# Projections kept in DRAM: pieces of 256 tokens split into pieces of 128, and the slot stores issued from ScalarE

## The chip, the cores and the metric

One core of one Trainium2 chip runs the kernel. The metric is the device time of a run in microseconds (us). A time named "median" is that of repeated runs; the profile is of one further execution, recorded by the hardware profiler. The engines are TensorE (PE; its weight loads are PEld), VectorE (DVE), ScalarE (ACT), GpSimd (POOL) and SyncE (SP). SyncE here only issues DMAs; ScalarE and GpSimd can issue DMAs too. Each engine carries out its own instructions in the order of the program.

## The reference, cut to what matters

Four sequences ("elements", b = 0 to 3) of 1024 tokens with 256 features pass through two layers, each an attention and a feed-forward part, with a normalisation after each. The change touches the first attention only:

```
x = _layernorm(x + _L0_attn_ref(x, ...))          # 16 heads of 16 features
    qkv = einsum('bsc,oc->bso', x, w_qkv)         # the projections
    q = layer_norm(q); k = layer_norm(k)          # per head, then rotary positions
    out = softmax(q k^T / 4) v, then w_proj
x = _layernorm(x + _L0_ffn_ref(x, ...))
x = _layernorm(x + _L1_attn_ref(x, ...))          # causal, 8 heads
x = _layernorm(x + _L1_ffn_ref(x, ...))           # 16 experts, 2 per token, 512 slots each
```

The last part scatters token rows into expert slots; slots that no token fills must hold an empty row.

## The kernel before, in words

All data is float32. The first attention of an element is written as 64 *units* (`first_units`): four groups of four heads, 16 steps each. A step i computes scores of the current group (`Attend.head`, L459) and, side by side, scores of the next group for its row maxima only (`Maxima.head`, L435). Four heads of 16 features (padded to 32) share the array at a time. A unit has two sets of four such products; between them come the value products of the step before (L477), and at some steps four transposes (L426, L492). Each score tile takes one of six PSUM banks (pool `ps_s`). ScalarE frees a score bank by the exponential (L468), VectorE frees a maxima bank by a reduction (L438). A seventh bank (`ps_m`, one buffer) serves transposes and all other products of this stage.

The order of the work is written by hand. `weave(units, n, pieces, big, mid, at, side, ...)` runs through the units, and behind each unit it does, in this order: `tick()`, which runs steps that were put off by `later(n, fn)` for n ticks; one step of `side`; then as many of `pieces` as bring `done` up to `total * (u + 1) // n`. From unit `at` on an entry of `mid` takes the place of the pieces once. For the first element (b = 0) this call has

- as units the 64 of `first_units(0)`;
- as pieces two empty ones and then the *stash*: the projections of elements 1, 2 and 3, which are made here and kept in DRAM until their turn. `stash_qk(b, pr)` makes queries and keys of half the heads (pr 0 and 1), `stash_v(b)` the values of b = 2 and 3. Order: qk(1,0), qk(1,1), v(2), qk(2,0), qk(2,1), v(3), qk(3,0), qk(3,1), four pieces of 256 tokens each, 32 in all;
- as mid `load_heads(1, 0)` at unit 30, which loads kept projections back;
- as side `prep`, one step per unit: loads of x (units 0 to 7), small weight steps on VectorE (`geometric`, units 8 and 9), the empty rows (made at unit 11, stored to the slots of expert e at unit 15 + e by `empty_slots`, L1210; a further store to `acc_d` at unit 27, L1213), and three integer weights: load of wg at unit 28, GpSimd's conversions (L1155) at 30 to 33, wu at 34 and 36 to 39, wd at 40 and 42 to 45. The empty rows and all three integer weights share one buffer ("hT").

A stash piece loads its input (`load_xin`, L140, tile "xin" with two buffers) on SyncE's queue, makes eight product instructions of 128x256 (four matmuls; L299 for qk, L331 for v) in the bank of `ps_m`, and ScalarE copies the bank out (L307, L339). For qk, one tick later GpSimd squares the copy (L311), two ticks later VectorE sums it (L313), and three ticks after the fourth piece SyncE stores 1 MB of projections (L316) and 64 KB of sums (L317). The 1 MB tile "va1" has one buffer, the sums' tile has two. For v, one tick after each piece SyncE stores its 256 KB (L340); that tile has two buffers. SyncE's queue thus holds, in program order, input loads, stores that wait for ScalarE or VectorE, slot stores, and weight loads that wait for GpSimd. `load_heads` also puts eight steps of about 2.9 us (L357) on GpSimd, one per tick.

Of the kernel before, what the change touches and what calls it, by code (L numbers as in the profile page):

```python
# [10 lines left out]
F32 = mybir.dt.float32  # L11
# [8 lines left out]
P = 128  # L20
# [15 lines left out]
def postln_layers_kernel(ctx: ExitStack, tc: tile.TileContext, a: dict, out: bass.AP):  # L36
    nc = tc.nc
# [65 lines left out]
    with ExitStack() as main:  # L103
# [4 lines left out]
        act = main.enter_context(tc.tile_pool(name="act", bufs=1))  # L108
# [8 lines left out]
        def later(n, fn):  # L117
            due.append((now_at[0] + n, fn))
# [12 lines left out]
        def bank(name, big):  # L131

            if big:
                return ps_s.tile([P, 512], F32, tag="s", name=name)
            return ps_m.tile([P, 512], F32, tag="m", name=name)

        def load_xin(b, j, name):
            t = fa.tile([P, 2, 256], F32, tag="xin", bufs=2, name=f"xin{name}_{b}_{j}")
            lo = b * S + j * 256
            nc.sync.dma_start(t, a["xT"][:, lo : lo + 256].rearrange("(c p) n -> p c n", p=P))  # L140
            return t
# [140 lines left out]
        for b in range(1, B):  # L282
            v_d[b] = dram.tile([P, TB * C], F32, name=f"v_d{b}")
            for pr in range(2):
                qk_d[b, pr] = dram.tile([P, TB * 256], F32, name=f"qk_d{b}{pr}")
                ss_d[b, pr] = dram.tile([P, TB * 16], F32, name=f"ss_d{b}{pr}")

        def stash_qk(b, pr):
            kept = {}

            def piece(j, big):
                if j == 0:
                    kept["x"] = act.tile([P, TB * 256], F32, tag="va1", bufs=1, name=f"xs_{b}_{pr}")
                    kept["ss"] = act.tile([P, TB * 16], F32, tag="k1", bufs=G1, name=f"sss_{b}_{pr}")
                xin = load_xin(b, j, f"k{pr}")
                ps = bank(f"qk0_{b}_{pr}_{j}", big)
                for i in range(2):
                    for c in range(2):
                        nc.tensor.matmul(  # L299
                            ps[:, i * 256 : (i + 1) * 256],  # L300
                            xin[:, c, i * P : (i + 1) * P],
                            w0[:, c, pr * 256 : (pr + 1) * 256],
                            start=c == 0,
                            stop=c == 1,
                        )
                x = kept["x"][:, j * 512 : (j + 1) * 512]
                nc.scalar.copy(x, ps)  # L307

                def squares():
                    sq = act.tile([P, 512], F32, tag="q1", bufs=G1, name=f"sqs_{b}_{pr}_{j}")  # L310
                    nc.gpsimd.tensor_tensor(sq, x, x, ALU.mult)  # L311
                    ss = kept["ss"][:, j * 32 : (j + 1) * 32]
                    later(1, lambda: nc.vector.tensor_reduce(ss, sq.rearrange("p (h d) -> p h d", d=D0), AX.X, ALU.add))  # L313

                def store():
                    nc.sync.dma_start(qk_d[b, pr], kept["x"])  # L316
                    nc.sync.dma_start(ss_d[b, pr], kept["ss"])  # L317

                later(1, squares)
                if j == 3:  # L320
                    later(3, store)

            return [lambda big, j=j: piece(j, big) for j in range(4)]

        def stash_v(b):
            def piece(j, big):
                xin = load_xin(b, j, "v")
                ps = bank(f"v0_{b}_{j}", big)
                for i in range(2):
                    for c in range(2):  # L330
                        nc.tensor.matmul(  # L331
                            ps[:, i * 256 : (i + 1) * 256],
                            xin[:, c, i * P : (i + 1) * P],
                            w0[:, c, 512:768],
                            start=c == 0,
                            stop=c == 1,
                        )
                x = act.tile([P, 512], F32, tag="nmT", bufs=2, name=f"vs_{b}_{j}")
                nc.scalar.copy(x, ps)  # L339
                later(1, lambda: nc.sync.dma_start(v_d[b][:, j * 512 : (j + 1) * 512], x))  # L340

            return [lambda big, j=j: piece(j, big) for j in range(4)]

        def load_heads(b, pr):

            xr = fa.tile([P, TB, 2, 8, D0], F32, tag="xr", bufs=1, name=f"xr_{b}_{pr}")
            ss = fa.tile([P, TB, 2, 8], F32, tag="ss", bufs=1, name=f"ss_{b}_{pr}")
            heads[b, pr] = (xr, ss)
            flat = ss.rearrange("p t s h -> p (t s h)")
            nc.sync.dma_start(flat, ss_d[b, pr])  # L350
            nc.sync.dma_start(xr.rearrange("p t s h d -> p (t s h d)"), qk_d[b, pr])

            def roots(k):
                if k == 0:
                    nc.gpsimd.tensor_scalar(flat, flat, D0 * 1e-6, None, ALU.add)
                p = flat[:, 16 * k : 16 * k + 16]
                nc.gpsimd.tensor_tensor(p, p, neg_half.to_broadcast([P, 16]), ALU.pow)  # L357

            for k in range(8):
                later(1 + k, lambda k=k: roots(k))  # L360
# [644 lines left out]
        def first_units(b):  # L1005

            oq0[b] = act.tile([P, TB, C], F32, tag="oq", bufs=2, name=f"oq0_{b}")
            last = None
            for g in range(G0):
                n = 4 * b + g  # L1010
                at = Attend(groups[n], oq0[b])
                mx = groups.get(n + 1)
                for i in range(16):
                    for hp in range(2):

                        then = []
                        for j in range(2):
                            if mx is not None:
                                then += [at.head(i, 2 * hp + j), mx.head(i, 2 * (1 - hp) + j)]
                            elif hp == 0:  # L1020
                                then += [at.head(i, 2 * j), at.head(i, 2 * j + 1)]
                        for fn in then:
                            fn()
                        if hp == 0:
                            if i > 0:
                                at.values(i - 1)
                            elif last is not None:
                                last.values(15)
                            if i == 3:
                                groups[n].turn(0, 1, name="a")  # L1030
                            if i == 5 and last is not None:
                                last.unload(1)
                            if i == 10 and mx is not None:
                                mx.turn(0, 0, name="a")
                            if i == 11:
                                at.unload(0)
                            if i >= 12 and n + 2 in groups:
                                groups[n + 2].turn((i - 12) // 2, i % 2)
                    if i == 0:
                        groups[n].close(1)  # L1040
                    if i == 3 and n + 2 < G0 * B:
                        nb, ng = divmod(n + 2, G0)
                        groups[n + 2] = Maxima(nb, ng, both_pool)
                    if i >= 4 and n + 2 in groups:
                        groups[n + 2].rotate(4)
                    if i == 8 and mx is not None:
                        mx.close(0)
                    yield
                last = at
            last.values(15)  # L1050

            def end(big):
                last.unload(1, big)

            ends[b] = end
# [145 lines left out]
        def empty_slots(e):  # L1201
            if e < 0:
                empty["z"] = z = act.tile([P, ECH, ROW], F32, tag="hT", bufs=1, name="empty")
                nc.gpsimd.memset(z, 0.0)
                none = act.tile([P, ECH], I32, tag="v_none", bufs=1, name="none")
                nc.gpsimd.iota(none, pattern=[[P, ECH]], base=N, channel_multiplier=1)
                nc.gpsimd.tensor_copy(z[:, :, ROW - 1].bitcast(I32), none)
            elif e < EM:
                to = disp_d[e * CAP : (e + 1) * CAP, :].rearrange("(c p) d -> p c d", p=P)
                nc.sync.dma_start(to, empty["z"])  # L1210
            else:
                rest = acc_d[N : N + CAP, :].rearrange("(c p) d -> p c d", p=P)
                based.append(nc.sync.dma_start(rest, empty["z"][:, :, 0:C]).ins)  # L1213
# [36 lines left out]
        for b in range(1, B):  # L1250
            stash += (stash_v(b) if b > 1 else []) + stash_qk(b, 0) + stash_qk(b, 1)
        weave(
            first_units(0), 64, [wait, wait] + stash, False, [lambda big: load_heads(1, 0)], 30, [f for f in prep if f], 0
        )
        flush()
        straight(project_v(1))
# [261 lines left out]
```

## Time and profile before

| | us |
|---|---|
| median of 3 runs | 2520.82 (2514.46 to 2523.96) |
| the profiled execution | 2506.56 |
| its span, first to last instruction | 2504.9 |
| TensorE busy in it | 2362.7 (94%) |
| VectorE, ScalarE, GpSimd busy | 1327.1, 1022.9, 740.7 |
| units of the first element, second value products to last | 95.95 to 410.68 |

In a timeline a line holds the start, the time until the end of the last instruction merged into it, the engine (SPq is SyncE's queue), the source line, the operation, the tile written and the tiles read, the shape, how many instructions were merged (x8), and in brackets the idle time before it with what ended it. Products overlap, since four of the small ones share the array, so their starts say more than their lengths.

In the stretch from 95 to 412 us the costliest groups of instructions are the maxima and score products (L435, L459), 503 records each; VectorE is busy 59% of the time from 95.95 to 410.68 and ScalarE 55% (186.82 and 172.40 of 314.73).

### The profile page before, as it was taken

Reading aid. Unit: us, or ns where it says so; the run is one execution under the profiler, and the core shown is the slowest. Engines: PE = TensorE matmul, PEld = TensorE weight load, DVE = VectorE, ACT = ScalarE, POOL = GpSimd, SP = SyncE. Lnnn points to the kernel's source line nnn. Section 1 sums busy time; section 2 is a strip of 40 time slices with the busy share of each in tenths; the row PEclk is TensorE's granted clock in tenths of the full one; section 3 lists DMA queues with packets and bytes.
Section 4 is the critical chain, followed back from the end, with each engine's and each line's share of the span. In section 5 each row is a group of like instructions: output and inputs, shape, how many; then the busy total and the mean of one; then the engine's idle time right before and its main releaser. Section 6 shows DMA issues by size and latency. Waiting matters only on the chain.

```text
span 2504.9 us, 36507 instructions
## 1 busy us (share of the span) xinstructions
PE 2362.7 (94%) x14452; PEld 1193.4 (48%) x14452; DVE 1327.1 (53%) x2945; ACT 1022.9 (41%) x2011; POOL 740.7 (30%) x1047
## 2 busy tenths in 40 slices
PE   6999999999999999999999999999999994999994
PEld 3333344444445544444455444445556443666662
DVE  6765554766656537687564566816534555111113
ACT  1355454555452345545524555462342340111112
POOL 5623622525124113454041320210111053112223
PEclk8999999999998999999989999999999895999997
DMA  3134223000000000001000000102000012444434
GB/s 88 34 112 134 70 68 100 1 27 1 1 1 27 2 1 1 23 30 48 31 1 1 1 1 1 52 18 98 1 1 1 1 52 68 101 101 118 103 89 145
DMA packets 79771, 109.89 MB, mean 44 GB/s; under 512 B 8944, under 2 KB 68592, under 8 KB 77936
## 3 DMA queue, kind: packets, MB, share of 16 engines
q1 hardware_dynamic: 54080, 80.21, 9.7%
q0 software_dynamic: 9984, 14.82, 3.1%
q10 hardware_dynamic: 15536, 12.53, 1.7%
q8 instruction: 113, 1.85, 0.3%
q14 instruction: 58, 0.48, 0.1%
HBM read 68.64 MB, written 38.90 MB: 43 GB/s over the span
## 4 chain that ended last, share of the span: by engine, by line
PE 85%; DVE 6%; POOL 4%; DMA 2%; issue 1%; ACT 1%; ACTq 0%; SPq 0%; POOLq 0%; DVEq 0%
PE sc L459 19%; PE av L477 9%; PE ph L1379 7%; PE py L1395 7%; PE gu L604 7%; PE sc L932 4%; PE mx L435 4%; PE mx L885 4%; PE p L852 4%; PE dn L620 3%; PE av L969 3%; PE dn L969 2%; PE ppa L568 2%; DVE part L896 2%; PE qk L299 2%; PE pt L426 1%
## 5 line engine op out<-in xcount | busy, mean ns | idle before, releaser
L438 DVE TENSOR_REDUCE part<-mx 128x1 f32<-128x512 f32 x1024 | 657.0, 685 | 355.0 <-PE mx L435 349.4
L468 ACT ACTIVATE pe<-sc 128x512 f32<-128x512 f32 x1024 | 554.0, 596 | 391.1 <-PE mx L435 333.3
L435 PE MATMUL mx<-kT,qT 32*128 32x512 f32 x2048 | 650.9, 641 | 5.3 <-DVE part L438 5.0
L459 PE MATMUL sc<-qT,kT 32*128 32x512 f32 x2048 | 614.1, 636 | 0.4 <-ACT pe L468 0.4
L459 PEld LDWEIGHTS sc<-qT,kT 32*128 32x128 f32 x2048 | 181.3, 183 | 223.1 <-issue 178.1
L477 PE MATMUL av<-pe,va 128*32 128x512 f32 x2048 | 272.7, 605 | 0.0
L896 DVE TENSOR_REDUCE part<-mx 128x1 f32<-128x512 f32 (+3 forms) x384 | 186.8, 549 | 154.5 <-PE mx L894 108.4
L435 PEld LDWEIGHTS mx<-kT,qT 32*128 32x128 f32 x2048 | 196.9, 184 | 53.9 <-DVE part L438 28.4
L943 ACT ACTIVATE pe<-sc 128x512 f32<-128x512 f32 (+3 forms) x384 | 157.4, 498 | 159.4 <-PE sc L932 158.9
L1379 PE MATMUL ph<-dmT,f 128*128 128x512 f32 x384 | 170.0, 601 | 4.4 <-DVE dmT L91 3.5
L946 POOL TENSOR_SCALAR_AFFINE_SELECT pe<-pe 128x256 f32<-128x256 f32 x128 | 52.2, 414 | 411.0 <-ACT pe L943 408.5
L1395 PE MATMUL py<-f,hTm 128*128 128x256 f32 x768 | 167.7, 379 | 0.0
L1387 ACT ACTIVATE hTm<-ph,b 128x512 f32<-128x512 f32 x96 | 60.7, 683 | 261.2 <-PE ph L1379 261.2
L1399 POOL DMA_INDIRECT acc_d<-yo,dm x48 | 74.6, 1554 | 284.6 <-DVE yo L1397 241.4
L1395 PEld LDWEIGHTS py<-f,hTm 128*128 128x128 f32 x768 | 145.9, 190 | 25.0 <-issue 5.7
L885 PE MATMUL mx<-kT,qT 32*128 32x512 f32 (+3 forms) x768 | 137.8, 593 | 6.7 <-DVE part L896 3.4
L357 POOL TENSOR_TENSOR ss<-ss,neg_half 128x16 f32<-128x16 f32 x48 | 138.9, 2906 | 0.5
L477 PEld LDWEIGHTS av<-pe,va 128*32 128x32 f32 x2048 | 40.3, 108 | 192.5 <-issue 183.4
L1396 DVE TENSOR_TENSOR yo<-py,b 128x256 f32<-128x256 f32 x48 | 20.4, 425 | 207.8 <-PE py L1395 207.8
L932 PE MATMUL sc<-qT,kT 32*128 32x512 f32 (+3 forms) x768 | 118.3, 541 | 1.6 <-DVE part L896 0.9
L1379 PEld LDWEIGHTS ph<-dmT,f 128*128 128x128 f32 x384 | 72.8, 192 | 94.7 <-issue 86.6
L604 PE MATMUL gu<-xTf,wg 128*128 128x256 f32 x384 | 106.8, 400 | 0.0
(342 smaller groups left out, 2892.9 us busy)
## 6 DMA issues: line engine op xcount, KB each, us to landing
f<-in_fc SPq DMA_DIRECT2D x14, 1024.0 KB, 5.0
f<-in_fc ACTq DMA_DIRECT2D x10, 1024.0 KB, 6.2
xink<-in_xT SPq DMA_DIRECT2D x32, 256.0 KB, 2.9
disp_d<-empty SPq DMA_DIRECT2D x12, 520.0 KB, 4.6
qk_d<-xs SPq DMA_DIRECT2D x6, 1024.0 KB, 3.9
xr<-qk_d SPq DMA_DIRECT2D x6, 1024.0 KB, 5.2
dm<-disp_d SPq DMA_DIRECT2D x11, 520.0 KB, 4.2
xinv<-in_xT SPq DMA_DIRECT2D x16, 256.0 KB, 3.7
```

What stands on the lines that cost most here:

```text
L435: nc.tensor.matmul(sc, self.qT[r, t * P : (t + 1) * P], self.kT[r, u * 512 : (u + 1) * 512], start=True, stop=True)
L438: return lambda: nc.vector.tensor_reduce(self.part[:, t, u, h : h + 1], sc, AX.X, ALU.max, negate=True)
L459: nc.tensor.matmul(sc, self.m.kT[r, kt * P : (kt + 1) * P], self.m.qT[r, qb * 512 : (qb + 1) * 512], start=True, stop=True)
L468: nc.scalar.activation(self.pes[i, h // 2][:, h % 2, :], sc, AF.Exp)
L477: nc.tensor.matmul(self.av[32 * h : 32 * h + 32, :], va0[:, kt, 4 * self.g + h, :], self.pes[i, h // 2][:, h % 2, :], start=kt == 0, stop= ...
L604: nc.tensor.matmul(ps[:, i * 256 : (i + 1) * 256], w[:, c, f * P : (f + 1) * P], xT[j][:, c, :], start=c == 0, stop=c == 1,)
L885: nc.tensor.matmul(scs[h][:, :n], qT[r, t * P : (t + 1) * P], kT[r, u * 512 : u * 512 + n], start=True, stop=not diag,)
L896: nc.vector.tensor_reduce(self.part[:, t, u, h : h + 1], scs[h][:, :n], AX.X, ALU.max, negate=True)
L932: nc.tensor.matmul(scs[h][:, off:], ones_h[r, :] if w else kT[r, kt * P : (kt + 1) * P], (self.m.nmT if w else qT)[r, q], start=w == 0, st ...
L943: nc.scalar.activation(pe[:, j, off:], scs[2 * hp + j][:, off:], AF.Exp)
L1379: nc.tensor.matmul(ph[:, i * CAP : (i + 1) * CAP], f1[:, c, (f + i) * P : (f + i + 1) * P], dmT[:, c, :], start=c == 0, stop=c == 1,)
L1395: nc.tensor.matmul(py[:, :C], hT[:, f, c * P : (c + 1) * P], f2[:, f, :], start=f == 0, stop=f == FF1 // P - 1)
```

## The change

Each stash piece is cut in two, of 128 tokens each. The first half loads the input for both; each half makes four product instructions in a bank of its own allocation and copies 256 columns out. Squares, sums and the stores follow the second half as before. The two empty pieces at the head of the list are gone, so the list has 64 pieces, and with `load_heads` 65 entries over 64 units. The stores of empty rows to the experts' slots are issued by ScalarE in place of SyncE.

```diff
+        def half(ps, xin, i, cols):
+            for c in range(2):
+                nc.tensor.matmul(
+                    ps[:, 0:256], xin[:, c, i * P : (i + 1) * P], w0[:, c, cols], start=c == 0, stop=c == 1
+                )
+
         def stash_qk(b, pr):
             kept = {}
 
-            def piece(j, big):
-                if j == 0:
+            def piece(j, i, big):
+                if (j, i) == (0, 0):
                     kept["x"] = act.tile([P, TB * 256], F32, tag="va1", bufs=1, name=f"xs_{b}_{pr}")
                     kept["ss"] = act.tile([P, TB * 16], F32, tag="k1", bufs=G1, name=f"sss_{b}_{pr}")
-                xin = load_xin(b, j, f"k{pr}")
-                ps = bank(f"qk0_{b}_{pr}_{j}", big)
-                for i in range(2):
...
+                if i == 0:
+                    kept["in"] = load_xin(b, j, f"k{pr}")
+                ps = bank(f"qk0_{b}_{pr}_{j}_{i}", big)
+                half(ps, kept["in"], i, slice(pr * 256, (pr + 1) * 256))
                 x = kept["x"][:, j * 512 : (j + 1) * 512]
-                nc.scalar.copy(x, ps)
+                nc.scalar.copy(x[:, i * 256 : (i + 1) * 256], ps[:, 0:256])
+                if i == 0:
+                    return
...
-            return [lambda big, j=j: piece(j, big) for j in range(4)]
+            return [lambda big, j=j, i=i: piece(j, i, big) for j in range(4) for i in range(2)]
 
         def stash_v(b):
...
+            def piece(j, i, big):
+                if i == 0:
+                    kept["in"] = load_xin(b, j, "v")
+                    kept["x"] = act.tile([P, 512], F32, tag="nmT", bufs=2, name=f"vs_{b}_{j}")
+                ps = bank(f"v0_{b}_{j}_{i}", big)
+                half(ps, kept["in"], i, slice(512, 768))
+                x = kept["x"]
+                nc.scalar.copy(x[:, i * 256 : (i + 1) * 256], ps[:, 0:256])
+                if i == 1:
+                    later(1, lambda: nc.sync.dma_start(v_d[b][:, j * 512 : (j + 1) * 512], x))
...
             elif e < EM:
                 to = disp_d[e * CAP : (e + 1) * CAP, :].rearrange("(c p) d -> p c d", p=P)
-                nc.sync.dma_start(to, empty["z"])
+                nc.scalar.dma_start(to, empty["z"])
...
         weave(
-            first_units(0), 64, [wait, wait] + stash, False, [lambda big: load_heads(1, 0)], 30, [f for f in prep if f], 0
+            first_units(0), 64, stash, False, [lambda big: load_heads(1, 0)], 30, [f for f in prep if f], 0
         )
```

More of the change, by code (lines that the diff above doesn't have):

```diff
@@ L286, in postln_layers_kernel @@
                 ss_d[b, pr] = dram.tile([P, TB * 16], F32, name=f"ss_d{b}{pr}")
+        def half(ps, xin, i, cols):
[3 more added lines that the diff above has]
+                )
         def stash_qk(b, pr):
             kept = {}
-            def piece(j, big):
-                if j == 0:
+            def piece(j, i, big):
+                if (j, i) == (0, 0):
                     kept["x"] = act.tile([P, TB * 256], F32, tag="va1", bufs=1, name=f"xs_{b}_{pr}")
                     kept["ss"] = act.tile([P, TB * 16], F32, tag="k1", bufs=G1, name=f"sss_{b}_{pr}")
-                xin = load_xin(b, j, f"k{pr}")
-                ps = bank(f"qk0_{b}_{pr}_{j}", big)
-                for i in range(2):
[L298 to L305, printed above, removed]
+                if i == 0:
+                    kept["in"] = load_xin(b, j, f"k{pr}")
+                ps = bank(f"qk0_{b}_{pr}_{j}_{i}", big)
+                half(ps, kept["in"], i, slice(pr * 256, (pr + 1) * 256))
                 x = kept["x"][:, j * 512 : (j + 1) * 512]
-                nc.scalar.copy(x, ps)
+                nc.scalar.copy(x[:, i * 256 : (i + 1) * 256], ps[:, 0:256])
+                if i == 0:
+                    return
                 def squares():
@@ L321, in piece @@
                     later(3, store)
-            return [lambda big, j=j: piece(j, big) for j in range(4)]
+            return [lambda big, j=j, i=i: piece(j, i, big) for j in range(4) for i in range(2)]
         def stash_v(b):
[L326 to L342, printed above, removed]
+            kept = {}
+            def piece(j, i, big):
[8 more added lines that the diff above has]
+                    later(1, lambda: nc.sync.dma_start(v_d[b][:, j * 512 : (j + 1) * 512], x))
+            return [lambda big, j=j, i=i: piece(j, i, big) for j in range(4) for i in range(2)]
         def load_heads(b, pr):
```

## Prediction

> **What bounds the kernel now.** I read the page first: its chain of work that ended last lies on TensorE.
>
> ```profile
> PE 85%; DVE 6%; POOL 4%; DMA 2%; issue 1%; ACT 1%; ACTq 0%; SPq 0%; POOLq 0%; DVEq 0%
> ```
>
> So the change is worth what it does to TensorE in the stretch that it touches, the 64 units of the first element, and "busy" does not say whether TensorE waits there. I therefore read TensorE's timeline unit by unit. Call a round the time from one unit's value products (L477) to the next one's: value products, four score and maximum heads, the unit's piece if it has one, four heads of the next unit.
>
> ```profile
> 112.75 1.06 PE L477 MATMUL av<-pe,va 128*32 128x512 f32 x8
> ...
> 114.82 1.99 PE L299 MATMUL qk<-w,xink 128*128 128x256 f32 x8
> ...
> 117.81 1.07 PE L477 MATMUL av<-pe,va 128*32 128x512 f32 x8
> ...
> 118.81 0.69 PE L459 MATMUL sc<-qT,kT 32*128 32x512 f32 x1
> ...
> 120.76 0.69 PE L435 MATMUL mx<-kT,qT 32*128 32x512 f32 x1
> ...
> 121.81 0.64 PE L477 MATMUL av<-pe,va 128*32 128x512 f32 x4
> ```
>
> A round with a piece takes 5.06 us (112.75 to 117.81), one without 4.00 (117.81 to 121.81), though the piece has 1.93 us of products. The plain round loses 0.87 us between its two sets of heads: eight heads follow each other and there are six banks ("s"). VectorE's timeline names the wait:
>
> ```profile
> 120.01 2.60 DVE L438 TENSOR_REDUCE part<-mx 128x1 f32<-128x512 f32 x4 [0.78 <-PE mx L435]
> ```
>
> The first reduction gives its bank back at 120.66, and the fourth head starts at 120.76. The 63 rounds from 95.95 to 410.68 last 314.73 us: 31 without a piece x 4.00 + 32 with x 5.06 = 285.9; 29 of them hold four transposes, 0.585 each, 17.0; 11.8 is left. Of that 10.1 belongs to input loads that came late (1.77, 1.00, 0.49, 6.39, 0.47 over the pattern), and 1.7 to VectorE and others. Two of the late loads show how it comes about. In SyncE's own timeline and TensorE's:
>
> ```profile
> 190.66 0.33 SPq L317 DMA_DIRECT2D ss_d<-sss  x1
> 191.26 0.32 SPq L340 DMA_DIRECT2D v_d<-vs  x1
> 191.63 0.42 SPq L1210 DMA_DIRECT2D disp_d<-empty  x1
> 192.15 0.52 SPq L140 DMA_DIRECT2D xinv<-in_xT  x1
> ```
> ```profile
> 196.08 1.97 PE L331 MATMUL v<-w,xinv 128*128 128x256 f32 x8 [1.74 <-DMA xinv<-in_xT]
> ...
> 292.59 3.53 PE L299 MATMUL qk<-w,xink 128*128 128x256 f32 x8 [4.79 <-DMA xink<-in_xT]
> ```
>
> SyncE works in order: the load for a piece stands behind the store of the last one, which waits for ScalarE's copy or VectorE's sums. That met TensorE where two pieces lay one unit apart with a store between; most lie two apart.
>
> **The change part by part.** 32 pieces become 64; the counter (65 items over 64 units) puts one behind every unit, heads' load at unit 30, two pieces behind unit 63.
>
> *TensorE.* Same products; half a piece is 4 x 0.241 = 0.97 us. In a plain round the banks come free 1.95 us after the first set began, and with half a piece the second set begins at 1.06 + 0.97 = 2.03: the hole is filled. The row for it is bounded from both sides: with 0.58 us of transposes in that place (432.17 to 436.17) a round still takes 4.00, with 1.93 it takes 5.06. I take 5.06 - 0.96 = 4.10. New sum: 61 x 4.10 + 4.00 + the last round 5.06 + 0.75 (its second half waits in the one bank "m" for the first one's copy) = 259.9. Gain 26.0.
>
> *ScalarE.* 32 copies of 585 ns become 64 of about 375 (the 128x256 copy, L858): 5.3 us more in all, beside TensorE: exponentials end 3.30 us into a round, the copy at 3.68, the next are due at 4.3. The 12 slot stores cost 0.37 to 0.48 each there (L1289, L1210), ahead of the copy: 4.13, still before 4.3. Price 0. At SyncE's worst, 1.38, it is 0.7 late and some 0.5 on TensorE, 12 x 0.5 = 6; below nothing it can't be for ScalarE. I take 0, since one store per unit doesn't pile up.
>
> *Moving those stores.* [...] By the row, a load alone lands after 2.7 us, behind one store of v and one of slots after 3.79, behind two of slots after 4.7. [...]
>
> *Loads moved closer to their stores.* Now a piece pair fills two units and the next pair's load always follows its predecessor's store by one unit. Behind a store of v: copy ends at 3.68 (4.13 with a slot store), 0.38 for the store, so the load goes out at 4.09 (4.54), lands 3.6 later (3.8), TensorE starts 0.14 after; it was due at 4.10 + 2.07, or 0.58 later where transposes lie ahead. Units 20, 22, 24: 2.2 each; 49: 1.7; 45, 47: 1.1 each; units 18 and 43 stand behind sums (end 4.09) and two stores: 2.6 and 1.9. Sum 15.0. Behind the qk stores at units 10, 35, 59: 4.55 + 3.0 against 6.75: 0.85 each, 2.6. Between 9 and 23 for all these, with landings from 2.7 to 4.7.
>
> *Weights.* The wg load waits for the last slot store; its follower at unit 28 is 0.6 late. GpSimd still makes the wu conversions late; what stood at unit 40 for 4.79 now hits unit 41, where I get 1.3 (0 to 5). Sum 1.9.
>
> *A new wait on ScalarE.* The tile "va1" has one buffer. The first half of the next head pair comes one unit after the last (two before), and its copy (now L307's successor) waits until the 1 MB store has landed (3.9). At units 8 and 57 that is 3.7 after the copy + 3.9 = 7.6, that is 3.5 into the next round: free. At unit 33 the store stands behind the wu load on SyncE, which waits for GpSimd's conversion until 1.15 into the round; it goes out at 1.63 and lands about 6.2 later (3.9 and the 2.2 that a weight load adds). Behind the waiting copy stand four exponentials of unit 34, and TensorE waits for their banks: 3.8. Between 0 and 6.
>
> *VectorE.* The geometric steps at units 8 and 9 (130.27 to 136.5) lose a long piece as cover: 1.0.
>
> Sum of waits: 15.0 + 2.6 + 1.9 + 3.8 + 1.0 = 24.3 against 10.1: 14.2 given back. Net 26.0 - 14.2 = 11.8 us. Later stages keep their work. The profiled execution took 2506.56 (span 2504.9 and 1.7 around it): 2494.8. The median of the three runs is 14.3 above that execution; the same 11.8 off it gives 2509.0.
>
> **Clock.** [...] Here, after 1.74 us idle the piece took 1.97, after 4.79 it took 3.53. [...]
>
> **The rivals.**
> A, likeliest (53%): hole filled, loads late: gain 4 to 18, 2503 to 2517.
> B (22%): loads land in time. SyncE has less in its queue once the slot stores leave it, and idle landings are 2.7; waits stay at the 10 of before: gain 26, 2495. Against it: the 1.74 above.
> C (12%): the hole stays. The copies and stores slow ScalarE so that banks come back later, rounds stay at 4.5 on average, and the late loads are all that is new: 14 lost, 2535. Against it: 0.6 us of slack on ScalarE per round.
> [...]
>
> **How the numbers follow.** 0.5%, 12.6 us, is about what a measurement of this kernel can tell from no change. A ends just under it: a fifth of the chance of all from A above 12.6 and B's 0.22 make 0.42 faster; A's rest and half of C and D make 0.46; 0.12 slower. The range leaves out about half of B's and the worse part of C and D: 2495 to 2527.
>
> **What would show it.** Right: rounds of 4.10 with four products of L299's kind in each; waits of TensorE for input loads summing to some 20 us at units 18 to 24 and 43 to 49; one wait of a copy on the qk store near unit 33; ScalarE issuing twelve stores at under 0.5. Wrong: rounds of 4.5 (C), waits under 10 (B), a granted clock of 0.5 in the middle of the stretch (D). The prediction fails most easily on the landing times, 1 us each being worth 12.

## The result, and the profile after

| | before, us | after, us | ratio, 95% interval |
|---|---|---|---|
| median, first comparison (4 and 4 runs) | 2521.11 | 2506.21 | 0.9944 (0.9917 to 0.9971) |
| median, repeated on one chip (59 and 22 runs) | 2511.29 | 2508.44 | 0.998 (0.9962 to 0.9998) |
| profiled executions, two each | 2506.56; 2516.25 | 2510.5; 2505.31 | |
| their 63 rounds, second to last value products | 314.73; 314.75 | 310.34; 308.98 | |

The first comparison came out 14.9 us shorter, close to the 11.8 of the prediction. The repetition, with many more runs, gives a ratio of 0.998, about 5 us (its medians lie 2.9 apart). The profiles side with the repetition: the stretch that the change touches lasts 314.7 us in both profiles of before and 4.4 and 5.8 less in the two of after. What follows the stretch is the same program in all kernels, and lasted between 2090 and 2107 us in the ten profiles of this study. So the sign was right, the sum was too favourable by a factor of two or more, and that the first comparison came so near it was luck. The rest of this text reads the stretch, where two executions of a kernel agree within 1.4 us.

The chain that ended last is still TensorE's, with a point less for it and one more for DMA:

```profile
PE 84%; DVE 6%; POOL 4%; DMA 3%; issue 1%; ACT 1%; ACTq 0%; SPq 0%; POOLq 0%; DVEq 0%
```

TensorE's timeline of a round after (value products, first heads, half a piece, second heads, the next value products; line numbers are 2 lower than before, and all the halves are on L290):

```profile
97.67 1.06 PE L475 MATMUL av<-pe,va 128*32 128x512 f32 x8
98.67 0.69 PE L457 MATMUL sc<-qT,kT 32*128 32x512 f32 x1
...
99.73 1.13 PE L290 MATMUL qk<-w,xink 128*128 128x256 f32 x4
100.80 0.69 PE L457 MATMUL sc<-qT,kT 32*128 32x512 f32 x1
...
101.87 1.06 PE L475 MATMUL av<-pe,va 128*32 128x512 f32 x8
```

The round lasts 4.20 us. Nothing waits in it: the first heads take from 98.67 to 99.73, the half piece from there to 100.80, and the second heads need 1.07, no more than the first. The hole that plain rounds had is filled. The gain of that was then spent. TensorE's waits from 91 to 412 us, first before, then after (engine, line, what it waited for, sum, times, longest):

```profile
PE qk L299 <- DMA xink<-in_xT: 5.2, 2, 4.8
PE v L331 <- DMA xinv<-in_xT: 3.1, 3, 1.7
PE sc L459 <- ACT pe L468: 0.4, 2, 0.2
```
```profile
PE v L290 <- DMA xinv<-in_xT: 7.2, 5, 1.9
PE qk L290 <- DMA xink<-in_xT: 5.1, 3, 2.3
PE sc L457 <- ACT pe L466: 3.4, 1, 3.4
PE v L290 <- DVE part L436: 1.4, 1, 1.4
PE v L290 <- ACT pe L466: 0.7, 1, 0.7
PE qk L290 <- ACT xs L306: 0.5, 1, 0.5
```

Before there were two long waits and a few short ones; after there are ten of 0.6 to 2.3 us for inputs and one of 3.4 for ScalarE. The two entries "<- DVE part" and "<- ACT pe" under v L290 are the pieces of units 43 and 47, where engines named had long been done; the early-load experiment below removes them, so they were loads too.

The first kind in SyncE's timeline, with TensorE's line under it:

```profile
174.35 0.34 SPq L318 DMA_DIRECT2D ss_d<-sss  x1
174.73 0.48 SPq L338 DMA_DIRECT2D v_d<-vs  x1
175.31 0.38 SPq L140 DMA_DIRECT2D xinv<-in_xT  x1
```
```profile
178.33 1.13 PE L290 MATMUL v<-w,xinv 128*128 128x256 f32 x4 [1.75 <-DMA xinv<-in_xT]
```

Round 18 began at 174.44. The load goes out 0.87 us into the round in which it is needed, because the sums' store and the store of v stand ahead of it and wait for the unit before.

The second kind, at units 33 and 34, in SyncE's, ScalarE's and TensorE's timelines:

```profile
251.54 0.37 SPq L1147 DMA_DIRECT2D wu_i<-in_wu  x1
251.96 0.46 SPq L317 DMA_DIRECT2D qk_d<-xs  x1
```
```profile
259.36 0.37 ACT L306 COPY xs<-qk 128x256 f32<-128x256 f32 x1 [5.53 <-DMA qk_d<-xs]
```
```profile
260.29 1.22 PE L457 MATMUL sc<-qT,kT 32*128 32x512 f32 x1 [3.43 <-ACT pe L466]
262.29 2.08 PE L290 MATMUL qk<-w,xink 128*128 128x256 f32 x4
```

The 1 MB store leaves only behind the wu load; ScalarE's copy into the one "va1" buffer waits 5.53 us for it to land, the exponentials queued behind the copy don't run, and TensorE stands for 3.43. Then the half piece takes 2.08 instead of 1.13: in the clock records TensorE had half its clock for 6.8 us from 259.3 on. That round took 11.51.

### The profile page after: what moved, and what is told of

It reads as the page before. It is cut to its first block, busy times and chain, and to the rows that moved or that the text cites. A ratio compares the mean times of both kernels' runs of the same rounds, so it can differ in the third digit from the quotient of the medians.

```text
span 2508.8 us, 36539 instructions
## 1 busy us (share of the span) xinstructions
PE 2356.0 (94%) x14452; PEld 1182.2 (47%) x14452; DVE 1329.8 (53%) x2945; ACT 1024.8 (41%) x2043; POOL 742.2 (30%) x1047
## 4 chain that ended last, share of the span: by engine, by line
PE 84%; DVE 6%; POOL 4%; DMA 3%; issue 1%; ACT 1%; ACTq 0%; SPq 0%; POOLq 0%; DVEq 0%
PE sc L457 19%; PE av L475 9%; PE ph L1377 7%; PE py L1393 7%; PE gu L602 7%; PE sc L930 4%; PE mx L883 4%; PE p L850 4%; PE dn L618 3%; PE mx L433 3%; PE av L967 3%; PE dn L967 2%; PE ppa L566 2%; DVE part L894 2%; PE qk L290 2%; PE pt L424 1%
## 5 line engine op out<-in xcount | busy, mean ns | idle before, releaser
L433 PE MATMUL mx<-kT,qT 32*128 32x512 f32 x2048 | 633.2, 648 | 5.3 <-DVE part L436 5.1
L457 PE MATMUL sc<-qT,kT 32*128 32x512 f32 x2048 | 596.9, 641 | 3.6 <-ACT pe L466 3.6
L457 PEld LDWEIGHTS sc<-qT,kT 32*128 32x128 f32 x2048 | 171.5, 184 | 217.5 <-issue 180.7
L433 PEld LDWEIGHTS mx<-kT,qT 32*128 32x128 f32 x2048 | 187.9, 186 | 40.5 <-DVE part L436 25.6
```

Of the source, the lines that this page charges most:

```text
L433: nc.tensor.matmul(sc, self.qT[r, t * P : (t + 1) * P], self.kT[r, u * 512 : (u + 1) * 512], start=True, stop=True)
L457: nc.tensor.matmul(sc, self.m.kT[r, kt * P : (kt + 1) * P], self.m.qT[r, qb * 512 : (qb + 1) * 512], start=True, stop=True)
```

## The experiments

Each was run beside the kernel before on one chip (two sets of four). "Stretch" is the time from the second value products of the first element to its last, 63 rounds, in the profiled execution.

**The kernel before, once more.** No edit.

> The kernel before once more, for a second profile and more times. My theory: the gain lies in the 64 units of the first element, and the two profiles compared so far show only 4.4 us of it there (314.7 against 310.3 us from the second value products to the last) because the profile of before was a quick execution; if the timed executions lose more in that stretch, its 63 rounds come out above 318 us here. Rival: the stretch repeats at 314.7 within 1 us, and what the medians differ by beyond 4.4 us is half-clock windows that fall differently in later stages. Both: ratio 1.000 within 0.003.

Ratio 0.9998 (0.9981 to 1.0016), stretch 314.75. The rival holds: the stretch repeats to 0.02 us, so the first comparison's 14.9 was not hidden in it. What follows the stretch took 2094.2 us in one profile and 2105.0 in the other.

**The changed kernel, once more.** No edit.

> The changed kernel once more. My theory: ratio 0.995 (0.9975 to 0.992), rounds of 4.20 us, one wait of TensorE of about 3.4 us at unit 34, a 63-round stretch of 308 to 313 us. Rival (chance alone made the median 14.9 us shorter): ratio 0.998 or more.

Ratio 0.998 (0.9962 to 0.9998), on the line that I had drawn for the rival; rounds of 4.20, one wait of 3.5 us at unit 34, stretch 308.98. Most of the first 14.9 did not come back; what the traces show is 4 to 6.

**The halves alone.**

```diff
-                nc.scalar.dma_start(to, empty["z"])
+                nc.sync.dma_start(to, empty["z"])
```

> The change without its second part: halves of pieces, but the slot stores stay in SyncE's queue. My theory: the halves carry the gain, the stores in front of the loads of units 18 to 24 add 0.5 to 1.5 us to each of four waits, so 2 to 5 us longer than the whole change. Rival (the move of the stores is what helps): as slow as before or slower.

Ratio 0.9998 (0.9981 to 1.0014), stretch 317.70: 7.4 to 8.7 us longer than the whole change, not 2 to 5, and 3 longer than before. This is one profile, of an execution (2524.02) near the slowest of its runs; the medians of this kernel and of the whole change, 2512.17 and 2508.44, lie 3.7 apart and their intervals overlap. So the times alone don't tell the two apart, and what follows is read from the traces. SyncE's timeline at unit 24, and TensorE's:

```profile
211.66 0.33 SPq L338 DMA_DIRECT2D v_d<-vs  x1
212.05 1.97 SPq L1208 DMA_DIRECT2D disp_d<-empty  x1
214.12 0.45 SPq L140 DMA_DIRECT2D xink<-in_xT  x1
```
```profile
218.00 2.08 PE L290 MATMUL qk<-w,xink 128*128 128x256 f32 x4 [3.64 <-DMA xink<-in_xT]
```

A slot store now stands between each store of v and the load. The waits of units 18, 20, 22, 24 are 3.33, 2.40, 2.56, 3.64 (after: 1.75, 1.95, 0.91, 2.16), and the last piece takes 2.08 as the one at half clock in after did, so that came on top. Measured from the start of its round, the load goes out 0.4, 0.5, 0.7 and 2.0 us later than after; from load to product takes 1.15 and 0.9 longer in units 18 and 22, the same in 20, and 0.6 less in 24. Together 5.2, the difference of the waits (11.9 against 6.8).

**The moved stores alone.** In the kernel before:

```diff
-                nc.sync.dma_start(to, empty["z"])
+                nc.scalar.dma_start(to, empty["z"])
```

> Only the second part: whole pieces of 256 tokens as before, slot stores from ScalarE. My theory: only the two late loads at units 21 and 25 (1.77 and 1.00 us) get shorter, and the wait for the slot stores at the wg load too; 1 to 3 us less than before, ratio 0.999. Rival (the stores in SyncE's queue are what costs): 10 us or more less, ratio 0.996 or lower.

Ratio 0.9983 (0.9963 to 1.0002), which doesn't tell it from no change; stretch 312.78, 2.0 less, as expected. The wait of 1.74 us at unit 21 became 0.47 and the one at unit 25 went. ScalarE took 0.366 to 0.387 us for each store, and TensorE shows no new wait worth a microsecond. So in the profiles the two parts of the change need each other: stores alone 2 us, halves alone a loss of 3, together a gain of 4 to 6. The times show neither part alone to differ from before.

**The change with early loads.** The next pair's load is issued behind the second half of the pair before, one unit earlier and ahead of the waiting stores. `ahead` lists the loads in order, `take_in` hands out what `next_in` has loaded, and `stash_v` is changed alike:

```diff
+        def next_in():
+            if ahead:
+                loaded_in.append(ahead.pop(0)())
...
-                    kept["in"] = load_xin(b, j, f"k{pr}")
+                    kept["in"] = take_in()
...
                 if i == 0:
                     return
+                next_in()
```

> The changed kernel, with each pair's input load issued one unit earlier (behind the second half of the pair before, so ahead of the stores that wait). My theory: the late loads go, all but the one behind the wd load; the 63-round stretch falls from 309-310 to 290-296 us, the hold on the 1 MB store at unit 33 stays at 3.4 us idle. Time ratio 0.991. Rival (the waits only move, since the transfers and not their place in the queue are slow): stretch over 302.

Ratio 0.9906 (0.9886 to 0.9925), stretch 294.47. One load wait is left, 1.6 us at unit 41 behind the wd load; the hold at unit 34 is still there (4.3 idle, 12.43 for the round). So the place in the queue made the loads late, not the transfers.

**The kernel before with early loads.** The same in whole pieces.

> The kernel before, whole pieces, with the same earlier loads. My theory: its waits behind stores (1.77, 1.00, 0.47) go and the one behind the wd load stays; the hole between the sets of heads in rounds without a piece stays, so the stretch is 310 to 313 us, some 18 longer than halves with early loads. Rival (halves fill nothing, only the loads count): as short as the halves with early loads, within 3 us.

Ratio 0.9958 (0.9942 to 0.9975), stretch 304.58, 10.15 under before. I expected 310 to 313, since I left the wait behind the wd load in place; the early load passes that too, as pieces lie two units apart. The 10.15 is the 10.1 that the prediction had summed as this kernel's load waits. Rounds without a piece still take 4.00 and those with one 5.06.

**The wu load one unit later.**

```diff
         wu, steps = dequant("wu", "wu", 2, 0.5 / 127.0)
-        prep += steps
+        prep += [lambda: None] + steps
```

> The changed kernel with the wu load (and the weight steps behind it) one unit later, so that the 1 MB store of unit 32's piece stands ahead of it in SyncE's queue. My theory: ScalarE's wait for that store goes, and with it TensorE's stop and the half clock of unit 34, 7.3 us; stretch 302 to 304. Rival (the store itself is slow to land, or the wait is of something else): ScalarE still waits over 3 us there and the stretch stays at 308 or more.

Ratio 0.996 (0.9948 to 0.9972), stretch 305.96, some 3 to 4.4 less, not 7.3. ScalarE's wait for the store is gone, and round 34 is an ordinary one. But the wu load now stands between the sums' store and the load of unit 35, whose wait is 3.17, with slower products behind it (heads of 1.22 and 1.06 us, as at half clock in after, where 0.69 and 0.59 are usual):

```profile
259.68 0.34 SPq L318 DMA_DIRECT2D ss_d<-sss  x1
260.12 0.38 SPq L1147 DMA_DIRECT2D wu_i<-in_wu  x1
260.60 0.94 SPq L140 DMA_DIRECT2D xink<-in_xT  x2
```

The cause of the hold was right; moving it aside in the same queue made the next one late.

**All of it.** Halves, early loads, the 1 MB store one unit after its last half (`later(1, ...)`), the sums' store as before, the wd load one unit later.

> Halves, early loads, the 1 MB store one unit after the last half instead of three, the wd load one unit later. My theory: 61 x 4.20 + 4.0 + 4.7 + 17.0 and about 2 of VectorE's: stretch 282 to 287, 28 to 32 us under before; time ratio 0.988. Rival: the half-clock windows or GpSimd's backlog become the limit and the stretch stays over 293.

Ratio 0.9883 (0.9862 to 0.9905), 2479.66 against 2509.53 us: faster than both kernels. TensorE's only recorded wait between 91 and 381.5 us is for the copy between the two halves at the last unit:

```profile
PE qk L290 <- ACT xs L318: 0.5, 1, 0.5
```

The stretch by window, for the change, for before with early loads, and for this kernel (start:end, length, TensorE busy and instructions, its weight loads, VectorE, ScalarE, GpSimd, granted clock, DMA share, GB/s):

```profile
97.67:408.01 310.34, 292.07 (x1884) 107.68 (x1881) 189.91 (x320) 174.70 (x345) 117.19 (x155) 0.98 0.26 86
```
```profile
97.34:401.92 304.58, 304.09 (x1885) 121.84 (x1885) 186.84 (x320) 172.48 (x313) 117.29 (x155) 1.00 0.27 86
```
```profile
96.92:381.20 284.28, 283.82 (x1884) 105.63 (x1880) 189.66 (x320) 174.06 (x345) 117.41 (x155) 1.00 0.30 94
```

The last two differ in the size of the pieces and in the places of some stores and one weight load, and TensorE waits for neither loads nor stores in them: 20.3 us is what the filled hole is worth, but for 0.4: VectorE and ScalarE held rounds 3, 9 and 44 for 1.7 in the one, VectorE rounds 9 and 10 for 1.3 in the other. "Busy" does not show the hole: before with early loads TensorE is busy in 304.09 of 304.58 us. In a plain round of that kernel the second heads start by ones and twos as banks come free, in place of four at a time, and each starts before the ones ahead of it have ended:

```profile
99.31 0.59 PE L475 MATMUL sc<-qT,kT 32*128 32x512 f32 x1
99.73 0.59 PE L451 MATMUL mx<-kT,qT 32*128 32x512 f32 x1
99.73 1.10 PE L475 MATMUL sc<-qT,kT 32*128 32x512 f32 x2
100.28 0.69 PE L451 MATMUL mx<-kT,qT 32*128 32x512 f32 x1
```

## Why the prediction was right or wrong

**What bounds the kernel.** Right. The stretch's 314.7 us were split into rounds, transposes, 10.1 us of late loads and 1.7 of others; taking the loads away gave 10.15. The split has two slips that cancel: 31 rounds hold transposes, not 29, and the last round, which has no heads of a next unit, is 1.07 shorter than taken.

**The hole.** Right in mechanism, 6.1 us too large. A round is 4.20, not 4.10: half a piece occupies 1.06 between the two sets of heads, not the 0.96 that was taken, while a whole one takes 1.92 (114.82 to 116.74 in before). Two halves cost 2.12. The term that was mis-sized is "half the products, half the time"; there are about 0.2 us per pair of halves more, 61 x 0.10 = 6.1. The gain from rounds was 26.0 - 6.1 = 19.9; the experiments measure 20.3, of which 0.4 is VectorE's and ScalarE's.

**Unit 0.** Missing from the sum. From its first heads to the second value products 4.90 us passed before (91.05 to 95.95) and 5.84 after (91.83 to 97.67): the first half piece is not hidden there, 0.94.

**The last unit.** Two halves, 5.31 us against 4.58: 0.73 where 0.75 was predicted.

**Late loads.** Right in mechanism and place. Over the pattern, units 18, 20, 22, 24: 1.82, 2.02, 0.98, 2.72 (predicted 2.6, 2.2, 2.2, 2.2); 43, 45, 47, 49: 1.45, 1.63, 0.72, 2.93 (1.9, 1.1, 1.1, 1.7). Sum 14.3 against 15.0; about 1 of it, in units 24 and 49, is half clock behind the wait, and the idle time alone is 12.8, not the "some 20" that the prediction named as a sign. Behind the qk stores 0, 0, 0.63 (10, 35, 59) against 2.6 in all; unit 35's cost nothing, as unit 34 had just stood still. Unit 28 was free (0.6 predicted), unit 41 1.66 (1.3).

**ScalarE's hold.** Right in place and cause, 7.3 instead of 3.8. From the store's issue to the copy that it holds 7.4 us passed (251.96 to 259.36) where I took 6.2. The idle time itself, 3.43, is near the 3.8. Of the 3.9 that are left, TensorE's work at half clock from 260.29 on (5.8 us) makes some 2.9.

**VectorE.** 0.84 at unit 9 and 0.45 at unit 10, predicted 1.0. The second stays 0.45 in the kernels with early loads, so it is not a load: in unit 10 the first reduction starts only at 138.21, behind the geometric steps, and the fourth of the heads waits for its bank until 138.94:

```profile
137.69 0.59 DVE L1183 TENSOR_TENSOR w1q<-w1q,wdir 128x24 f32<-128x24 f32 x1
138.21 1.28 DVE L436 TENSOR_REDUCE part<-mx 128x1 f32<-128x512 f32 x2
```
```profile
138.47 0.69 PE L433 MATMUL mx<-kT,qT 32*128 32x512 f32 x1
...
138.94 0.69 PE L433 MATMUL mx<-kT,qT 32*128 32x512 f32 x1
```

Before lost 1.25 at unit 9 for the same steps, so nothing was added.

**The clock.** The sum has no term for it, and here it failed. In after the granted clock was 0.50 for 3.41 us from 211.51 and from 341.21, behind waits of 2.16 (unit 24) and 2.34 (unit 49), slowing rounds 25 and 50 by 1.1 each, and for 6.83 us from 259.29, in the wait of 3.43 at unit 34. That is 13.7 us at half clock, so at most 6.8 lost, an estimate: half of it. In the second profile of the change slower products followed a wait of 1.74 (unit 18: the half piece took 1.66 in place of 1.13, the heads 1.22 in place of 0.69), while one of 2.15 there (unit 24) and one of 1.95 in the first (unit 20) passed unpunished. So a wait of about 2 us can be enough here, and need not be.

**Sum.** 19.9 of gain (with the last unit's 0.73 already in it) less the waits (loads 14.3, 0.6 and 1.7, the hold 7.3, VectorE 1.3, half clock in rounds 25 and 50 2.2; 27.3 before rounding) over the pattern, where before had 11.8: 19.9 - 15.5 = 4.4, which is the stretch of the profile (314.73 - 310.34). With unit 0, 3.5. The prediction's 11.8 became 4.4 by 6.1 for the halves, 3.5 for the hold and 2.2 for half clocks; 4.4 came back, 2.9 from loads that were less late than I had them and the rest from 1.7 us of VectorE's and other waits before, which I had not set against those after. The 3.5 is for the most part the clock's too.

**Moving the stores.** Priced at nothing by itself. Free for ScalarE, right. But in the one profile without it the move is worth 7.4 to 8.7 us, where loads follow stores by one unit. The four later issues make 3.7 of it; 1.5 are later landings, net, behind a slot store in the same queue. In that profile units 18 to 25 are 8.3 longer than in the first of after, 3.1 more than their waits; the heads are slower in three places (1.21 and 1.05 us from 181.0, 1.04 to 1.06 from 193.7, 1.22 from 220.0, against 0.69 and 0.59), in after in one. If each lasts the 3.41 us of the one in after, the two more can cost up to 1.7 each, half of that, an estimate. That fits, but was not tested alone.

**The rivals.** C fell: rounds are 4.20. No run shows D, half clock behind every late load, which the chances count: in the profile of after it followed two of the ten waits for inputs, and came with the hold. B fell, as the loads came late; with early loads added the gain in the stretch is 20.3, with the other moves 30.4. A, the likeliest, held: 4.4 and 5.8 lie at the low end of its 4 to 18.

**Left open.** Why the medians of the first comparison lie 14.9 apart. What follows the stretch, equal in all kernels, varied by 17 us between profiles. The time at half clock in it varied too, 164.5 us in before and 174.2 in after: by half of the difference, an estimate, up to 4.8 of the 6.6 between these two. The remainder I don't know.

## What to carry to other kernels

Filler between two bursts that share a ring of banks cost here only what it was longer than the wait that it covered (a round took 4.00 us without a piece, 4.20 with half a one, 5.06 with a whole one): cut it to the size of the hole, and add what the cut costs (here about 0.1 us per half). When work is cut finer, look at every queue that its loads share with waiting stores: a load that had two units of lead has one, and is late by what its queue waits for. Issue loads before the stores of the work ahead; here that turned a gain of 5 us into one of 24, and with the one-buffer tile's store moved up too, into 30.

## What the runs showed of the hardware

These are two stretches of 3.42 us in after, around the waits of units 20 and 24, and the one behind the second. TensorE's busy time stands behind the length; the last three figures are the granted clock, the DMA share and GB/s:

```profile
187.61:191.03 3.42, 1.70 (x12) 0.99 (x12) 1.12 (x2) 1.30 (x3) 3.19 (x7) 1.00 0.60 204
208.09:211.51 3.42, 1.59 (x8) 0.99 (x12) 1.11 (x3) 1.20 (x3) 0.00 (x0) 1.00 1.06 368
211.51:214.92 3.41, 3.41 (x20) 0.72 (x16) 1.29 (x2) 1.09 (x3) 0.00 (x0) 0.50 0.12 40
```

TensorE stood idle for 1.72 us of the first (its wait of 1.95 began before it), and the granted clock stayed at 1.00 until 211.51; for 1.83 of the second (of a wait of 2.16), and 0.50 followed for 3.41 us. Two other profiles, read by the lengths of the heads (0.69 and 0.59 us mostly, 1.22 and 1.06 at half clock in after), show no clear order: 0.69 and 0.59 behind waits of 2.15 (the change once more, unit 24) and 2.56 (halves alone, unit 22), but 1.22 behind one of 1.74 (the change once more, unit 18), and 0.86, then 1.05 behind one of 1.23 (halves alone, unit 41). What decides is not shown.

With the halves alone, SyncE took 0.42 to 1.97 us to issue a 520 KB slot store that ScalarE issued in 0.366 to 0.387 each time; bytes and count are the same, and what else differs, as far as the traces show, is what stood in the queue.
